# Binding the expert units' loads, and reads at the end, to the landing of earlier additions in a two-layer decoder kernel

## The chip, the core and the metric

The kernel runs on one core of a Trainium2 chip. A core has a matrix engine (TensorE, PE), a vector engine (VectorE, DVE), a scalar engine (ScalarE, ACT), GpSimd (POOL) and a sequencer for transfers (SyncE, SP). Each works through its own instructions in order, and they wait for each other and for transfers by semaphores. Transfers (DMAs) are issued by SP, ACT or POOL and are all carried out by the core's 16 DMA engines. The metric is the time of one execution on the device in microseconds; lower is better. The figure compared is the median of unprofiled runs.

## The reference, cut to what matters

The program is a decoder of two layers on 32 sequences of 100 tokens with 256 features (3,200 rows in all). Each layer has a self-attention, a cross-attention to a context and a mixture of experts. The change lies in the last of these stages, the mixture of experts of layer 1:

```
def _moe_forward(hidden_states, gate_weight, e_bias, w1, w2, w3, shared_gate, shared_up, shared_down):
    ...
    topk_idx, topk_w = _route(x, gate_weight, e_bias)          # 8 of 64 experts for each row
    ...
    xe = jnp.zeros((E, CAP, H), x.dtype).at[sorted_e, pos].set(tok_sorted, mode='drop')   # CAP = 256
    h = jax.nn.silu(jnp.einsum('ech,efh->ecf', xe, w1)) * jnp.einsum('ech,efh->ecf', xe, w3)
    ye = jnp.einsum('ecf,ehf->ech', h, w2)
    ...
    out = jax.ops.segment_sum(vals * flat_w[:, None], flat_t, num_segments=T)
    shared = jax.nn.silu(x @ shared_gate.T) * (x @ shared_up.T) @ shared_down.T
    return (out + shared).reshape(B, S, H)
```

An expert takes at most 256 rows; each of its outputs is weighted and added to the row that it came from. A shared part works on all rows. The kernel's output is the residual plus both.

## The kernel before, in words

**Units.** While layer 1's cross-attention ends, the routing puts each row into its place for each of its experts: POOL scatters rows, with their number and weights behind the 256 features (321 numbers, `XROW`), into `x1_d` in DRAM, 256 places to an expert (L1818). A list of the experts in use is computed (`listi`). Then `units` (L1992) works through 32 units in the order of that list: units 0 to 23 (`WHOLE`) are an expert's 256 places in two halves of 128, units 24 to 31 are the first half alone. What is left, if anything, is worked through by a second call behind a branch (L1921); it is not entered with this input.

**A unit's steps.** SP loads the expert's weights (`weights`, L1999 to L2003, 384 KB into a tile `we`, 12 of them) and its rows (`rows`, L2005 to L2016, 321 KB into a tile `xe`, 8 of them; half of that for a half unit). PE turns the rows (`expert_turn`, L2061), multiplies by the two first weights (`expert_hidden`), and two units later by the last one (`expert_add`); DVE writes the weighted result to a tile `ye` (L2109, 6 of them, each free again once its addition has landed), and POOL issues one indirect transfer for each half, which adds 128 rows of 256 numbers to a sum in DRAM (L2113). These are called additions here. There are 2 x 24 + 8 = 56.

**Two sums.** Additions go to two sums in DRAM in turn, even units to the first (`sum_d[0]`), odd ones to the second; the last three units, 29 to 31, all go to the second. An addition waits until those of the unit before on the same sum have landed, since two units may hold the same row (`self.depend(got, added.get(side, []), ...)`). The two halves of one unit don't wait for each other.

**The order of work.** The loop of `units` writes PE's order by hand: in step i it turns unit i, computes the hidden part of unit i-1, takes some steps of the shared part, and finishes unit i-2. SP's loads run ahead of it: weights 0 to 3, rows 0 to 4, weights 4 to 8 and rows 5 go first, and step i begins with rows i+6 and weights i+9. SP works in order; a load waits for a free tile, and for the eighth load before it, because eight semaphores go round. Rows also wait for `self.flag` (L1915), which says that the scatter has landed.

**The end.** x, the residual with the shared part, lies in SBUF as 25 tiles of 128 rows. When the units are done, each sum is read back in five chunks of five tiles (640 KB each, L1938), into `xnT` for the first sum and `wA` for the second, and DVE adds each chunk to x (L1941); after a chunk of the second sum ACT stores that part of x to the output (L1943). The chunks of the first sum wait for its last addition (unit 28), those of the second for `end`, a small POOL instruction (L2052) that waits for the last additions of both.

Of the kernel before, what the change touches and what calls it, by code (L numbers as in the profile page):

```python
# [13 lines left out]
ALU = mybir.AluOpType  # L14
# [6 lines left out]
NF = NT // P  # L21
# [100 lines left out]
class Kernel:  # L122
# [1764 lines left out]
    def l1_ffn(self):  # L1887
        nc, tc, a = self.nc, self.tc, self.a
        x = self.x
        with ExitStack() as st:  # L1890
            self.psum = st.enter_context(self.banks("l1f", s=3, t=3, m=2))
            pool = st.enter_context(tc.tile_pool(name="p1f", bufs=2))
            ep = st.enter_context(tc.tile_pool(name="e1f", bufs=2))

            self.wbs = self.wts.tile([P, 3584], F32, tag="wB", name="wB2")
            steps, route = self.shared, self.last_route
            with tc.manual_schedule(engines={mybir.EngineType.PE}):
                next(steps)
                next(steps)

                (used, _), = self.routes
                next(used)
                next(route)
                us = next(steps)
                next(used)
                next(route)
                us += next(steps)
                next(used)
                for _ in route:
                    pass  # L1910
                while us < FIRST1:
                    us += next(steps)

            flag = pool.tile([1, 1], F32, tag="flag", name="flag", bufs=2)
            self.flag = nc.gpsimd.memset(flag, 0.0)  # L1915
            self.depend(self.flag, self.sent1, "all rows are in their places")
            whole, first, second = (0, 1), (0,), (1,)
            units = [(u, whole) for u in range(WHOLE)] + [(u, first) for u in range(WHOLE, UNITS)]
            end, first = self.units(ep, units, steps)
            n = nc.values_load(self.listi[0:1, 2 * E1 : 2 * E1 + 1], min_val=0, max_val=E1)  # L1920
            with tc.If(n > 0):  # L1921
                units = [(u, second) for u in range(WHOLE, UNITS)] + [(u, whole) for u in range(UNITS, E1)]
                more, _ = self.units(ep, units)

                word = pool.tile([1, 1], F32, tag="word", name="word")
                branch = nc.sync.dma_start(word, self.sum_d[1][0:1, 0:1])
                self.depend(branch, [more.ins], "the units' sums")


            ends = [self.xnT.rearrange("p k n -> p (k n)"), self.wa1[:, : NF * D]]  # L1930
            ends = [t.rearrange("p (f d) -> p f d", f=NF) for t in ends]
            sums = [t.rearrange("(f p) d -> p f d", p=P) for t in self.sum_d]
            out = a["out"].rearrange("b t d -> (b t) d").rearrange("(f p) d -> p f d", p=P)

            for i, others in enumerate((first, [end.ins])):
                for f in range(0, NF, 5):
                    at = slice(f, f + 5)
                    got = nc.sync.dma_start(ends[i][:, at, :], sums[i][:, at, :])  # L1938
                    self.depend(got, others + [branch.ins], "the last sums")
                    tc.declare_no_dep(got.ins, group="behind", reason="SyncE has waited in the branch")  # L1940
                    nc.vector.tensor_tensor(x[:, at, :], x[:, at, :], ends[i][:, at, :], ALU.add)  # L1941
                    if i == 1:
                        nc.scalar.dma_start(out[:, at, :], x[:, at, :])  # L1943

    def shared1(self, first):

# [45 lines left out]
    def units(self, pool, units, beside=None):  # L1992

        nc, tc = self.nc, self.tc
        we, xes, xTs, hTs, added, tags = {}, {}, {}, {}, {}, {}
        self.after = None
        n_all = len(units)

        def weights(i):  # L1999
            we[i] = pool.tile([P, 768], F32, tag="we", name="we", bufs=12)  # L2000
            u = units[i][0]
            e = nc.sync.value_load(self.listi[0:1, E1 + u : E1 + u + 1], min_val=0, max_val=E1 - 1)
            nc.sync.dma_start(we[i], self.a["wexp"][bass.ds(e, 1)].rearrange("o p n -> p (o n)"))  # L2003

        def rows(i):  # L2005
            u, halves = units[i]
            t = xes[i] = pool.tile([P, 2, XROW], F32, tag="xe", name="xe", bufs=8)
            e = nc.sync.value_load(self.listi[0:1, u : u + 1], min_val=0, max_val=E1)
            if len(halves) == 2:
                at = self.x1_d.rearrange("(e s p) d -> e p s d", p=P, s=2)[bass.ds(e, 1)]  # L2010
                got = nc.sync.dma_start(t, at.rearrange("o p s d -> p (o s) d"))
            else:
                at = self.x1_d.rearrange("(e s p) d -> s e p d", p=P, s=2)[halves[0]][bass.ds(e, 1)]
                got = nc.sync.dma_start(t[:, 0, :], at.rearrange("o p d -> p (o d)"))
            if beside:
                self.depend(got, [self.flag.ins], "all rows are in their places")  # L2016

        with tc.manual_schedule(engines={mybir.EngineType.PE}):
            room = -3.0
            for i in range(4):  # L2020
                weights(i)
            for i in range(5):
                rows(i)
            for i in range(4, 9):
                weights(i)
            rows(5)
            for i in range(n_all + 2):
                if i + 6 < n_all:
                    rows(i + 6)
                if i + 9 < n_all:  # L2030
                    weights(i + 9)
                if i < n_all:
                    self.expert_turn(pool, i, len(units[i][1]), xes, xTs)
                if 0 <= i - 1 < n_all:
                    self.expert_hidden(pool, i - 1, len(units[i - 1][1]), we[i - 1], xTs, hTs)

                if beside and i < WHOLE:
                    room += 0.65
                    while room > 0:
                        took = next(beside, None)  # L2040
                        if took is None:
                            break
                        room -= took
                if 0 <= i - 2:
                    side = int(not beside or i % 2 == 1 or i - 2 >= n_all - 3)
                    self.expert_add(pool, i - 2, units[i - 2], we.pop(i - 2), tags, hTs, added, side, beside)
                if i < n_all:
                    tags[i] = self.expert_tags(pool, units[i], xes.pop(i))
            for _ in beside or ():
                pass  # L2050
        flag = pool.tile([1, 1], F32, tag="flag", name="flag_u", bufs=2)
        flag = nc.gpsimd.memset(flag, 0.0)  # L2052
        self.depend(flag, added.get(0, []) + added[1], "the units' sums")
        return flag, added.get(0)

    def expert_turn(self, pool, i, n, xes, xTs):
        nc = self.nc
# [181 lines left out]
```

## Time and profile before

| what | value |
|---|---|
| median of 3 unprofiled runs | 2843.68 us (2843.59 to 2845.27) |
| the profiled execution's own time | 2870.41 us |
| its span, first to last instruction | 2868.6 us |
| PE busy | 2756.2 us (96%) |
| DVE, ACT, POOL busy | 1773.2, 1391.4, 765.4 us |
| moved by the DMAs | 241.86 MB, 84 GB/s on average |
| `we` loads | 32, 384 KB each |
| `xe` loads | 24 of 321 KB, 8 of 160.5 KB |
| additions to the sums | 56, first POOL start 2717.35 us, last 2841.81 us |
| reads of the sums, stores of the output | 5 + 5 and 5, 640 KB each |

The profile is of one execution, with microseconds from the span's start. A line of a timeline gives start, duration, engine, source line, operation, tiles written and read, how often, and in brackets how long the engine sat idle before it and what ended that wait. SPq is the queue of SP's transfers; its durations are those of issuing, not of moving. In a table of stretches the columns are the stretch, its length, busy time (and instructions) of PE, of its weight loads, of DVE, ACT and POOL, then the granted clock of PE, the mean busy share of the DMA engines and GB/s. The chain that ended last is followed back from the last instruction to whatever released each step.

### The profile page before, as it was taken

The numbers are of one execution on the slowest core, as the hardware profiler recorded it, in microseconds if no ns is written. First come the engines' busy times: TensorE is split into PE (matmuls) and PEld (weight loads), VectorE is DVE, ScalarE is ACT, GpSimd is POOL, SyncE is SP. The second block draws the span as 40 slices with busy tenths as digits, with TensorE's granted clock in tenths as the row PEclk, the third lists the DMA queues.
The fourth block names the chain that finished last, engine by engine and source line by source line (L and its number), as shares of the span: only waits on it lengthen the run. The fifth ranks groups of instructions, "written<-read, shape, count | busy, mean of one in ns | idle before, by whom it ended". The sixth has DMA issues, their size and how long they took to land. (4 is left out here: it accounts for less than half of the span.)

```text
span 2868.6 us, 64252 instructions
## 1 busy us (share of the span) xinstructions
PE 2756.2 (96%) x24856; PEld 2133.5 (74%) x24856; DVE 1773.2 (62%) x5205; ACT 1391.4 (49%) x4210; POOL 765.4 (27%) x960
## 2 busy tenths in 40 slices
PE   8999999999999899999999999999999999999893
PEld 7888888777777656888886777777777777776582
DVE  7666766687888732222226877667676666776453
ACT  5554645677767511222223226556565556567120
POOL 3222212332222243222221230021211302223464
PEclk9999999999999899999999999999999999999997
DMA  7444333000000033665552210010000000000396
GB/s 249 131 134 162 133 141 120 22 16 16 16 16 16 10 124 125 199 210 207 197 201 87 79 42 9 7 50 21 18 15 9 15 9 14 10 11 6 96 269 161
DMA packets 133867, 241.86 MB, mean 84 GB/s; under 512 B 40714, under 2 KB 105925, under 8 KB 126768
## 3 DMA queue, kind: packets, MB, share of 16 engines
q1 hardware_dynamic: 103488, 143.53, 15.9%
q0 software_dynamic: 26784, 90.83, 9.8%
q8 instruction: 200, 3.28, 0.5%
q10 hardware_dynamic: 3280, 3.28, 0.3%
q14 instruction: 115, 0.94, 0.1%
HBM read 152.12 MB, written 111.18 MB: 92 GB/s over the span
## 5 line engine op out<-in xcount | busy, mean ns | idle before, releaser
L1818 POOL DMA_INDIRECT x_d<-xr,slot x200 | 194.9, 975 | 670.4 <-ACT eT L844 591.0
L178 PE MATMUL ps_t<-xnT,wA 128*128 128x200 f32 (+1 forms) x1608 | 321.9, 347 | 1.6 <-DMA wA<-in_wq 1.0
L178 PE MATMUL ps_t<-cT,q 128*128 128x361 f32 (+1 forms) x832 | 307.3, 472 | 0.0
L844 ACT COPY eT<-ps_t 124x384 f32<-124x384 f32 x400 | 191.2, 486 | 225.1 <-PE ps_t L843 219.6
L178 PEld LDWEIGHTS ps_t<-xnT,wA 128*128 128x128 f32 x1608 | 272.5, 191 | 30.1 <-issue 14.5
L834 ACT ACTIVATE wBx<-ps_t,m 128x361 f32<-128x361 f32 x400 | 227.4, 569 | 119.6 <-DVE m L831 109.2
L178 PE MATMUL ps_t<-xT,w 128*128 128x256 f32 (+1 forms) x1276 | 260.2, 363 | 0.7 <-ACT xT L172 0.7
L590 DVE TENSOR_REDUCE m<-ps_t 100x1 f32<-100x361 f32 x512 | 239.7, 524 | 19.3 <-PE ps_t L178 19.1
L178 PEld LDWEIGHTS ps_t<-xT,w 128*128 128x128 f32 x1276 | 223.6, 190 | 36.2 <-issue 9.3
L831 DVE TENSOR_REDUCE m<-ps_t 128x1 f32<-128x361 f32 x400 | 210.6, 527 | 60.3 <-PE ps_t L178 56.9
L843 PEld LDWEIGHTS ps_t<-ident,wBx 128*124 128x124 f32 x1200 | 150.2, 139 | 117.7 <-issue 70.7
L612 ACT ACTIVATE e<-ps_t 121x300 f32<-121x300 f32 x512 | 173.9, 426 | 123.1 <-PE ps_t L178 123.1
L384 ACT ACTIVATE e<-s,m 100x100 f32<-100x100 f32 x512 | 185.6, 364 | 66.2 <-DVE m L378 66.1
L843 PE MATMUL ps_t<-ident,wBx 128*124 128x128 f32 x1200 | 196.8, 275 | 3.6 <-DVE top L1758 2.3
L388 POOL TENSOR_TENSOR e<-e,rz 100x400 f32<-100x400 f32 x128 | 109.3, 855 | 323.7 <-PE ps_t L178 195.4
L178 PE MATMUL ps_t<-wA,cT 128*124 128x512 f32 x384 | 194.5, 594 | 0.0
L1465 DVE TENSOR_TENSOR h<-ps_t,g 128x256 f32<-128x256 f32 (+1 forms) x145 | 58.1, 402 | 188.6 <-ACT g L1464 178.8
L836 DVE TENSOR_SCALAR wBx<-wBx,sums 128x361 f32<-128x361 f32 x400 | 165.6, 414 | 9.4
L178 PEld LDWEIGHTS ps_t<-q,k 32*121 32x121 f32 x3072 | 129.0, 182 | 33.5 <-issue 7.1
L855 PEld LDWEIGHTS ps_t<-eT,v 124*64 124x64 f32 x3072 | 134.9, 137 | 15.2 <-issue 8.1
L1464 ACT ACTIVATE g<-ps_t 128x256 f32<-128x256 f32 (+1 forms) x145 | 52.8, 365 | 191.0 <-PE ps_t L178 165.9
L835 DVE RECIPROCAL sums<-sums 128x1 f32<-128x1 f32 x400 | 63.7, 159 | 126.0 <-ACT wBx L834 123.6
(335 smaller groups left out, 5500.9 us busy)
## 6 DMA issues: line engine op xcount, KB each, us to landing
x_d<-fill SPq DMA_DIRECT2D x16, 1284.0 KB
we<-in_wexp SPq DMA_DIRECT2D x32, 384.0 KB
cT<-in_ctxT SPq DMA_DIRECT2D x64, 186.0 KB
xe_d<-zero SPq DMA_DIRECT2D x8, 1028.0 KB
xe<-x_d SPq DMA_DIRECT2D x24, 321.0 KB
sum<-fill SPq DMA_DIRECT2D x10, 640.0 KB
yk<-y_d SPq DMA_DIRECT2D x25, 256.0 KB
xe<-xe_d SPq DMA_DIRECT2D x24, 257.0 KB
```

The lines of the kernel that those rows point to most:

```text
L178: self.nc.tensor.matmul(out, lhsT=l, rhs=r, start=(i == 0), stop=(i == n - 1))
L384: nc.scalar.activation(t[:, i, :], s[:, i, :], AF.Exp, bias=m[:, i : i + 1], accum_out=rz[:, i : i + 1])
L388: nc.gpsimd.tensor_tensor(t[:, h, :], t[:, h, :], self.last(rz[:, h], T), ALU.mult)
L590: got = nc.vector.tensor_reduce(m[:, j, o : o + 1], ps[r], AX.X, ALU.max, negate=True)
L612: nc.scalar.activation(t[:, r], ps[r].rearrange("p (c t) -> p c t", c=NKC), AF.Exp)
L831: self.after = nc.vector.tensor_reduce(m, ps, AX.X, ALU.max, negate=True)
L834: nc.scalar.activation(t, ps, AF.Exp, bias=m, accum_out=z)
L836: nc.vector.tensor_scalar(t, t, z, None, ALU.mult)
L843: nc.tensor.transpose(pt[:, c, :], es[n % 5][:, c * KC : (c + 1) * KC], self.ident)
L844: self.after = nc.scalar.copy(eT[:, :, o : o + P], pt)
L855: nc.tensor.matmul(pz[64 * j : 64 * j + 64, i, :], lhsT=v[:, c, h * 64 : (h + 1) * 64], rhs=eT[:, c, o : o + T], start=(c == 0), stop=(c = ...
L1818: got = nc.gpsimd.indirect_dma_start(out=self.x1_d[:, :], out_offset=bass.IndirectOffsetOnAxis(ap=slot[:, j, k : k + 1], axis=0), in_=xr[: ...
```

## The change

The loads move to the end of a step and run less far ahead: after unit i-2 is finished, step i issues rows i+5 and weights i+6 (before: rows i+6 and weights i+9, at the step's beginning). Weights 6 to 8 and rows 5, which were issued before the loop, are now issued in it. Rows i also wait for the landing of the additions of unit i-7, weights i for those of unit i-8, where there is such a unit. `units` returns the additions of every unit (`landed`) in place of those of the first sum's last unit.

At the end the ten reads come in another order: chunks 0, 1, 2 of the first sum, chunks 0, 1, 2 of the second, then chunk 3 of the first, 3 of the second, 4 of the first, 4 of the second. The first three wait for the landing of units 28, 29 and 30 respectively, all others for `end`. PE's, ACT's and POOL's instructions stay the same in number and order; DVE's and ACT's at the end follow the reads.

```
-            end, first = self.units(ep, units, steps)
+            end, landed = self.units(ep, units, steps)
+            open_at = [landed[len(units) - i] for i in (4, 3, 2)]
...
-            for i, others in enumerate((first, [end.ins])):
-                for f in range(0, NF, 5):
-                    at = slice(f, f + 5)
-                    got = nc.sync.dma_start(ends[i][:, at, :], sums[i][:, at, :])
-                    self.depend(got, others + [branch.ins], "the last sums")
-                    tc.declare_no_dep(got.ins, group="behind", reason="SyncE has waited in the branch")
-                    nc.vector.tensor_tensor(x[:, at, :], x[:, at, :], ends[i][:, at, :], ALU.add)
-                    if i == 1:
-                        nc.scalar.dma_start(out[:, at, :], x[:, at, :])
+            open_at += [[end.ins]] * 7
+            order = [(0, 0), (0, 1), (0, 2), (1, 0), (1, 1), (1, 2), (0, 3), (1, 3), (0, 4), (1, 4)]
+            for (i, f), others in zip(order, open_at):
+                at = slice(5 * f, 5 * f + 5)
+                got = nc.sync.dma_start(ends[i][:, at, :], sums[i][:, at, :])
+                self.depend(got, others + [branch.ins], "the last sums")
+                tc.declare_no_dep(got.ins, group="behind", reason="SyncE has waited in the branch")
+                nc.vector.tensor_tensor(x[:, at, :], x[:, at, :], ends[i][:, at, :], ALU.add)
+                if i == 1:
+                    nc.scalar.dma_start(out[:, at, :], x[:, at, :])
...
         def weights(i):
...
-            nc.sync.dma_start(we[i], self.a["wexp"][bass.ds(e, 1)].rearrange("o p n -> p (o n)"))
+            got = nc.sync.dma_start(we[i], self.a["wexp"][bass.ds(e, 1)].rearrange("o p n -> p (o n)"))
+            self.depend(got, landed.get(i - 8, []), "not in front of earlier units' sums")
...
         def rows(i):
...
             if beside:
                 self.depend(got, [self.flag.ins], "all rows are in their places")
+            self.depend(got, landed.get(i - 7, []), "not in front of earlier units' sums")
...
-            for i in range(4, 9):
+            for i in range(4, 6):
                 weights(i)
-            rows(5)
             for i in range(n_all + 2):
-                if i + 6 < n_all:
-                    rows(i + 6)
-                if i + 9 < n_all:
-                    weights(i + 9)
                 if i < n_all:
                     self.expert_turn(pool, i, len(units[i][1]), xes, xTs)
...
                     self.expert_add(pool, i - 2, units[i - 2], we.pop(i - 2), tags, hTs, added, side, beside)
+                    landed[i - 2] = added[side]
+                if i + 5 < n_all:
+                    rows(i + 5)
+                if i + 6 < n_all:
+                    weights(i + 6)
                 if i < n_all:
                     tags[i] = self.expert_tags(pool, units[i], xes.pop(i))
...
-        return flag, added.get(0)
+        return flag, landed
```

## The prediction

> **What bounds the kernel now.** I read the page first (TensorE, PE, is busy 96% of the span, so only a stage where PE waits can give time back), then the busy time by stretches for the last 150 us, then GpSimd's (POOL's) timeline there, the waits, SyncE's (SP's) own timeline, and the chain at the end. Stretches (PE, PEld, DVE, ACT, POOL busy, granted clock, DMA share, GB/s):
>
> ```profile
> 2721.00:2764.00 43.00, 42.71 (x209) 35.14 (x208) 25.19 (x73) 11.63 (x24) 27.88 (x18) 1.00 1.08 318
> 2764.00:2795.00 31.00, 31.00 (x162) 26.66 (x161) 19.32 (x57) 8.99 (x19) 22.59 (x15) 1.00 0.94 212
> 2795.00:2828.00 33.00, 22.39 (x123) 18.10 (x122) 13.39 (x49) 5.48 (x17) 27.05 (x18) 0.90 0.45 56
> 2828.00:2846.40 18.40, 2.37 (x11) 1.73 (x10) 7.76 (x9) 0.00 (x0) 6.36 (x5) 0.63 0.60 184
> 2846.40:2868.60 22.20, 0.00 (x0) 0.00 (x0) 8.60 (x6) 0.00 (x0) 0.00 (x0) 0.50 0.88 296
> ```
>
> PE works without a gap until 2795, then idles and its clock falls, while POOL is at its densest. The units end on POOL's additions. POOL's timeline:
>
> ```profile
> 2737.12 1.54 POOL L2113 DMA_INDIRECT sum<-ye,ids  x1 [2.25 <-DMA sum<-ye,ids]
> 2738.97 1.55 POOL L2113 DMA_INDIRECT sum<-ye,ids  x1 [0.30 <-DVE one L2090]
> 2755.85 1.54 POOL L2113 DMA_INDIRECT sum<-ye,ids  x1 [2.30 <-DMA sum<-ye,ids]
> ...
> 2812.70 1.55 POOL L2113 DMA_INDIRECT sum<-ye,ids  x1 [0.30 <-issue]
> ...
> 2834.73 1.54 POOL L2113 DMA_INDIRECT sum<-ye,ids  x1 [2.32 <-DVEq L1921]
> 2841.81 1.64 POOL L2113 DMA_INDIRECT sum<-ye,ids  x1 [5.53 <-DMA sum<-ye,ids]
> ```
>
> An addition takes POOL 1.55 + 0.30 = 1.85 us. Until 2790 every second unit waits longer: it waits for the landing of the addition before it on its sum (two sums, taken in turn). Afterwards POOL runs at 1.85. SP and the chain:
>
> ```profile
> 2720.88 0.38 SPq L2011 DMA_DIRECT2D xe<-x_d  x1
> 2768.13 0.38 SPq L2011 DMA_DIRECT2D xe<-x_d  x1
> 2787.16 8.24 SPq L2014 DMA_DIRECT2D xe<-x_d  x3
> 2833.24 5.02 SPq L1938 DMA_DIRECT2D xnT<-sum  x5
> 2846.35 4.00 SPq L1938 DMA_DIRECT2D wA<-sum  x5
> ```
> ```profile
> 2834.73 6.34 DMA sum<-ye,ids
> 2841.11 0.69 issue
> 2841.81 4.32 DMA sum<-ye,ids
> ...
> 2848.88 11.91 DMA wA<-sum
> 2860.88 1.49 DVE x_sb L1941
> ```
>
> The loads are all issued by 2795, far ahead of the additions, which end at 2845. Unit 30's addition then takes 6.34 us beside five reads of the first sum, and the last 22 us are transfers alone.
>
> **Landings.** The trace's DMA records give 144 packets to each addition on POOL's queue. From POOL's start to the last packet an addition took 6.0 to 6.8 us around 2730, 4.4 to 5.7 around 2780, 3.3 to 3.5 from 2797 on with no load in flight, 2.6 where few rows are valid (the half units). A weights packet takes 121 ns, a rows packet 56 ns; over 16 engines a unit's weights are 128 x 121 / 16 = 0.97 us, its rows 256 x 56 / 16 = 0.90. Over 42 additions (the fifth on) a straight line fits: latency = 3.41 + 0.89 x (engine time of load packets that start 1 to 5 us after POOL's start), to 0.45 us.
>
> **Part 1, the gates on rows and weights.** They bind. Rows 7 went out at 2720.88 and may now only follow unit 0's landing, 2725.94 in this trace; rows 23 went out at 2768.13 and must follow unit 16's, 2795.70. No instruction of PE, ACT or POOL changes; SP issues the same 64 loads, each now waiting for POOL's semaphores. Behind a waiting rows load on SP stands the next weights load, bound to the same landing, so nothing is held that was not held already.
>
> The pace of whole units follows from the chain on one sum: two units take 1.85 (first addition) + latency of the second + 1.4 (last packet to POOL's next start; 1.0 to 1.9 in the trace). With pace T a 4 us window holds 4/T units' loads: latency = 3.41 + 0.89 x 1.87 x 4/T. Both together give T = 4.14 us, latency 5.0. Before, units 2 to 16 took (2790.46 - 2727.76)/14 = 4.48 and units 16 to 24, with no loads about, 3.71, which is POOL's floor (2 x 1.85). The work of loading beside additions is not removed, it is spread; the gain is that the eight units at the floor no longer leave slack unused. At the start about two loads fewer are queued in front of unit 0, whose latency goes from 6.7 to about 5, so unit 2 starts near 2726.1. Unit 24 then starts at 2726.1 + 22 x 4.14 = 2817.2, before 2820.1: **-2.9 us**. Bounds: the floor of 3.71 from unit 5 (PE delivers it at 2738.3) gives 2808.8, -11.3; the early latency kept throughout (5.9) gives T = 4.58, 2826.9, +6.8. I take the fit's value, as it holds for both densities of loads.
>
> What it could cost on PE: a unit's turn needs its rows, issued about 1.0 us after the landing seven units back and landed some 4.5 us later; the result two units older follows 3.3 us after that turn. Result k is so ready at the earliest 16 us after the start of unit k-5, and is wanted 5 x 4.14 = 20.7 after it. 4 us of cover; a step of the shared part (3.4 us on PE) uses nearly all of it. I price it at 0; if the cover is gone, each shared step costs up to 3.4.
>
> Half units: in the trace, units 24 to 27 follow at 1.85 with latency 2.63 and 1.07 to the next start, exactly twice 1.85. Now loads of rows 27 to 31 (half size) and weights 28 to 31 fall here: 1.42 us of engine time per unit, latency +0.89 x 1.42 = +1.26 once on each sum, and some 0.5 more for unit 26: **+1.8 us** (0 to +4).
>
> A rule speaks against a gain here. The row: under loads an addition's first packet came 4.0 us after POOL's start, without them 2.1. The Trainium skill, "DMA: Bandwidth & Descriptors", section "Queues, rings and completion order", says that an engine alternates between its queues, finishing a packet of about 9 to 17 descriptors before it switches; so an addition waits for one such packet whether two loads are queued or five, and thinning the queue buys nothing while any load is in flight. By that the whole-unit term would be 0 in place of -2.9 and the total +4.8, an estimate from that page.
>
> **Part 2, the reads at the end.** Reads of chunks 0, 1, 2 of the first sum follow the landings of units 28, 29, 30; chunks 3 and 4 move behind the end. Beside unit 30's addition (before: first packet 4.13 us after POOL's start, when two chunks had gone by, last 5.71) there are still chunks 0 and 1; only the interleaving with chunk 2 goes, about 1.0. Unit 31's took 3.75 and has chunk 2 beside it: 0.2 less. **-1.2 us** (-3.0, both at 2.6 + 1.1, to +0.5). SP waits in order here, but behind these reads stand only those that wait for the end.
>
> After the end seven reads follow instead of five. The records show 343 packets a microsecond for reads from 2850 to 2856 and 377 for the stores until 2865, without a gap: 2 x 640 packets / 343 = 3.7 us more, and the last read, DVE's 1.49 and store stand further back, 0 to 0.9 more. **+4.2 us** (3.4 to 4.6). DVE's two moved additions (2 x 1.49) lie beside the transfers.
>
> **Sum**, on the profiled execution: -2.9 + 1.8 - 1.2 + 4.2 = +1.9, its span 2868.6 to 2870.5. That run took 2870.41, 1.8 around the span; the median of the unprofiled runs is 2843.68, 26.7 lower. I carry the difference over: **2845.6 us**. About 0.2% (5.7 us) is what a measurement of this kernel can tell from no change, so this is no change; its own range is 2840 to 2851.
>
> **Rivals.**
> (a) *The additions are freed*: POOL at its floor from unit 5. -11.3 + 0 - 1.2 + 4.2 = -8.3, **2835**. For: the latency falls to 3.4 as soon as loads end. Against: it needs second additions at 2 x 3.71 - 3.25 = 4.2 us, and none from unit 2 to 15 but one (3.66 at 2764.95, a first one) came under 4.3 with loads about. Chance 0.20.
> (b) *The loads collide with the very additions they wait for* (slower): a landing releases rows, weights and POOL's next unit on that sum at once, so both reach the DMA engines together, each time. Latency 5.9 as around 2740, T = 4.58, +9.7 against the forecast: **2855**. Each 0.1 us of latency costs 22 x 0.05 = 1.1 us, so it is slower than 0.2% from a latency of about 5.4. For: additions at 2766.80 and 2770.95, caught by three loads, took 5.4 and 5.7. Against: per unit the engines have 1.87 us of loads in over 4, so half of the additions should find them idle. Chance 0.25.
> (c) *The moved reads are hidden* under the stores: total -1.9, **2842**. Against it the gapless rates above. Chance 0.05. That the gates do nothing is excluded by the two issue times above.
>
> **How the numbers follow.** Forecast 0.50 (of it 0.37 within 0.2%, 0.10 slower, 0.03 faster), (a) 0.20 faster, (b) 0.25 slower, (c) 0.03 within and 0.02 faster. Together faster 0.25, same 0.40, slower 0.35. The range 2836 to 2856 takes in (a) nearly and (b) to its price, leaving 0.1 on each side.
>
> **What would show it.** Right: rows loads spaced about 4.1 us through to 2815; POOL waiting on DMA about as often at unit 22 as at unit 8; PE idle in small pieces from 2730 on; unit 24's addition at 2814 to 2820; seven reads and five stores in some 27 us after the last landing (23.0 before). Wrong: POOL at 1.85 steps under loads (a); latencies over 5.4 or PE waiting for xe (b); under 25 us after the last landing (c).

## The result, and the profile after

| what | before | after |
|---|---|---|
| median of 22 runs each | 2844.54 us | 2849.94 us |
| lowest and highest | 2841.70, 2850.53 | 2845.18, 2862.24 |
| ratio of after to before | | 1.0019, 95% interval 1.0011 to 1.0026 |
| profiled execution | 2870.41 us | 2851.53 us |

The change costs 5.4 us (3.1 to 7.4 by the interval): 0.19%, just inside the 0.2% that the prediction took for no change, though the 22 runs do tell it from nothing. The forecast was 2845.6, its range 2836 to 2856.

The two profiled executions can't be compared by their spans. The one before reaches the flag ahead of the units at 2705.18 us, the one after at 2679.34: 25.9 us apart ahead of anything that was changed. Runs of the kernel before on other chips show the same two levels (last section). So all that follows counts from POOL's start of unit 0's addition, and the sections between are:

| section | before | after | difference | predicted |
|---|---|---|---|---|
| unit 0 to unit 24 | 102.77 | 102.68 | -0.1 | -2.9 |
| unit 24 to unit 27 | 5.59 | 8.51 | +2.9 | +1.8 |
| unit 27 to the last landing | 19.84 | 19.44 | -0.4 | -1.2 |
| last landing to the end of the span | 22.99 | 27.70 | +4.7 | +4.2 |

POOL's starts and the span are read from timelines, landings from the DMA records (144 packets to an addition). The four differences add to +7.1 for two single executions; the medians say +5.4.

Busy time by stretches, after (columns as before: PE, its weight loads, DVE, ACT, POOL, granted clock, DMA share, GB/s):

```profile
2691.00:2735.00 44.00, 39.83 (x185) 32.88 (x184) 22.74 (x68) 10.85 (x22) 31.41 (x21) 0.92 0.91 217
2735.00:2766.00 31.00, 28.27 (x131) 22.64 (x130) 15.76 (x47) 7.42 (x16) 21.40 (x14) 0.96 0.92 210
2766.00:2799.00 33.00, 26.75 (x145) 22.54 (x143) 17.12 (x56) 7.58 (x20) 24.62 (x16) 0.89 0.86 201
2799.00:2822.10 23.10, 10.71 (x64) 8.88 (x64) 9.73 (x25) 1.85 (x6) 9.51 (x7) 0.83 0.43 117
2822.10:2849.80 27.70, 0.00 (x0) 0.00 (x0) 11.94 (x8) 0.00 (x0) 0.09 (x1) 0.50 0.84 285
```

The loads did what the change says: GB/s is even at 217, 210, 201 where it fell from 318 to 56 before. But PE, which was busy but for 0.3 us from 2721 to 2795 before, now idles in every stretch, and its granted clock is 0.92 and 0.96 in the first two, where it was 1.00 before. The last stretch is the end: transfers alone for 27.7 us.

What the engines waited for between unit 0 and the end of the units (engine, tile and line; total us, times, longest), first before, then after:

```profile
DVE ye L2109 <- DMA sum<-ye,ids: 17.4, 10, 3.2
POOL sum L2113 <- DMA sum<-ye,ids: 13.8, 7, 5.5
PE ps_t L2061 <- DMA xe<-x_d: 0.3, 1, 0.3
```
```profile
POOL sum L2117 <- DVE ye L2113: 21.1, 8, 12.0
PE ps_t L2065 <- DMA xe<-x_d: 13.9, 8, 4.8
POOL sum L2117 <- DMA sum<-ye,ids: 9.6, 4, 4.4
```

Before, DVE waited for a free `ye` tile: PE and DVE were so far ahead that they filled all six. That wait has gone (0.9 us is left), and in its place PE waits 13.9 us for rows. POOL waits less for landings and more for results: of its 21.1 us, 12.0 are the wait for unit 0, which is there before too. The results' lead over POOL (POOL's start less the end of DVE's write of that unit's `ye`) grew to 16 us by unit 24 before; after, it lies between 0 and 4 us at most units up to the 22nd. A result is called late here where POOL stood ready and started right behind the write of `ye`.

SP's, PE's and POOL's timelines, after, at the place where this lead runs out:

```profile
2716.68 0.60 SPq L2005 DMA_DIRECT2D we<-in_wexp  x1
2723.14 0.38 SPq L2014 DMA_DIRECT2D xe<-x_d  x1
```
```profile
2722.06 1.03 PE L178 MATMUL ps_m<-we,he 128*128 128x256 f32 x4
2727.26 1.08 PE L2065 MATMUL ps_t<-ident,xe 128*128 128x128 f32 x4 [4.17 <-DMA xe<-x_d]
```
```profile
2728.69 1.55 POOL L2117 DMA_INDIRECT sum<-ye,ids  x1 [0.30 <-issue]
2734.72 1.54 POOL L2117 DMA_INDIRECT sum<-ye,ids  x1 [4.48 <-DVE ye L2113]
...
2806.68 1.55 POOL L2117 DMA_INDIRECT sum<-ye,ids  x1 [0.30 <-issue]
2812.67 1.54 POOL L2117 DMA_INDIRECT sum<-ye,ids  x1 [4.44 <-DMA sum<-ye,ids]
2818.69 1.55 POOL L2117 DMA_INDIRECT sum<-ye,ids  x1 [4.48 <-DVE x_sb L1943]
```

Rows 12 went out at 2723.14, though unit 5, whose landing they are bound to, had landed at 2717.85. In SP's instructions, nine reads of list entries into registers (`value_load`, for this unit and for later ones) stand between weights 12 and rows 12: the scheduler, which orders SP, had put later units' reads in front of the load that waits. They fill the time from 2717.32 to 2722.80, 0.61 us for each. PE waits 4.17 us for these rows, the first turn after it takes 1.08 us where later ones take 0.44 in the chain, and unit 10's addition starts 4.18 us late. Rows 20 go out at 2757.81 in the same way, behind eight reads, though unit 13 had landed at 2753.42. The last three lines are the end: units 29, 30 and 31 follow each other at 6.0 us, where before it was 3.9 and 7.1.

The chain that ended last, after:

```profile
2723.14 3.98 DMA xe<-x_d
2727.26 1.08 PE ps_t L2065 x4
...
2757.81 4.40 DMA xe<-x_d
...
2806.68 5.26 DMA sum<-ye,ids
2811.95 4.53 DMA xnT<-sum
...
2829.51 14.16 DMA wA<-sum
```

It runs over PE and these two loads in the whole units, and at the end over unit 29's addition, a read of the first sum and the last reads of the second.

First theory (A): the parts add up. The end costs +4.7 less 0.4, the half units +2.9, and the whole units would have gained some 3 us had SP's register reads not made rows late. Rivals: the gates cost everything because the loads meet the additions they wait for (B); the gates gain and the end costs more (C); PE has too little cover whatever SP does (D); the additions' own latency sets the pace and PE's waits cost nothing (E).

### The profile page after: what moved, and what is told of

It is laid out like the page before. It is cut to its first block, busy times and chain, and to the rows that moved or that the text cites. A ratio compares the mean times of both kernels' runs of the same rounds, so it can differ in the third digit from the quotient of the medians.

```text
span 2849.8 us, 64259 instructions
## 1 busy us (share of the span) xinstructions
PE 2748.8 (96%) x24856; PEld 2129.8 (75%) x24856; DVE 1772.4 (62%) x5205; ACT 1392.4 (49%) x4210; POOL 765.2 (27%) x960
## 4 chain that ended last, share of the span: by engine, by line
PE 84%; DVE 8%; DMA 3%; ACT 2%; issue 2%; POOL 1%; SPq 0%; DVEq 0%; POOLq 0%; ACTq 0%
PE ps_t L178 59%; PE ps_t L855 5%; PE ps_t L843 5%; PE ps_t L1486 4%; PE ps_t L868 3%; DVE m L590 3%; PE ps_s L178 2%; PE ps_t L395 1%; PE ps_t L621 1%; PE ps_t L253 1%; PE ps_m L178 1%; DVE zd L636 1%; DMA sum<-ye,ids 1%; DMA wA<-sum 1%; DVE x_sb L1368 1%
```

## Experiments

Each run is compared with the kernel before on the same chip. e1 to e4 ran on one chip; e5 to e8, e9 and e10, and e11 and e12 ran on three others, where the kernel before takes 2870 to 2871 us, so ratios are compared, not times. A difference in us behind a ratio is worked out from the ratio, and can be up to 1.5 us away from the difference of the two medians. Profiles are of one execution each, and unit 24's start is counted from unit 0's.

**e1, the bound loads alone.** The end is that of before.

```
-            open_at = [landed[len(units) - i] for i in (4, 3, 2)]
+            first = landed[len(units) - 4]
...
-            for (i, f), others in zip(order, open_at):
+            for i, others in enumerate((first, [end.ins])):
+                for f in range(0, NF, 5):
```

> The bound loads of the change with the reads at the end as before. Theory A (the change adds up by its parts; in the two traces the units up to the 24th cost -0.1 us, the half units +2.9, the additions of units 30 and 31 -0.4, the transfers after them +4.7): about +2.9, that is some 2847.5 us beside 2844.5 before; 23 us from the last landing to the end of the span. Rival B (the gates themselves cost all of the +5.4, by loads that meet the additions they wait for, and the end costs nothing): +5 or more. Rival C (the gates gain what the prediction said, and the end costs more than 4.7): -1 to -3.

Measured: 2846.28 against 2846.38 us, ratio 1.0001 (0.9992 to 1.0011). The bound loads cost nothing and bring nothing, within 3 us. B falls with its 5 or more. The interval goes from -2.3 to +3.1 us, so these runs alone rule out neither A's +2.9 nor a small gain as in C; C falls by e2, where the end costs less than C's 7. Unit 24 starts at 100.85, units 24 to 27 take 8.69.

**e2, the end alone.** Loads as before, the ten reads in the order of after.

```
-            end, first = self.units(ep, units, steps)
+            end, landed = self.units(ep, units, steps)
+            open_at = [landed[len(units) - i] for i in (4, 3, 2)]
...
+            order = [(0, 0), (0, 1), (0, 2), (1, 0), (1, 1), (1, 2), (0, 3), (1, 3), (0, 4), (1, 4)]
```

> The loads as before, the order of the ten reads as after. Theory A: -0.4 and +4.7, so about +4 us, 2848.5; 27 to 28 us from the last landing to the end of the span. Rival B: within 1 us of before. Rival C: +7 or more.

Measured: 2849.28 against 2846.38, ratio 1.0011 (1.0002 to 1.0020), +3.1 us (0.6 to 5.7); from the last landing to the end 28.12 us, from unit 27 to the last landing 19.72 (19.84 before). The stretch behind the last landing, to be held against the last one of before in the prediction:

```profile
2819.40:2847.60 28.20, 0.00 (x0) 0.00 (x0) 11.94 (x8) 0.00 (x0) 0.09 (x1) 0.50 0.83 279
```

Of the two parts, only the end has a loss that can be told from nothing. e1 and e2 add to +3.4; the change has +5.4 with an interval that reaches down to 3.1, so some 2 us may belong to both together and stay unassigned.

**e3, SP in the order of the program.** The changed kernel, with each register read right in front of its own load.

```
-        with tc.manual_schedule(engines={mybir.EngineType.PE}):
+        with tc.manual_schedule(engines={mybir.EngineType.PE, mybir.EngineType.SP}):
```

> The changed kernel with SP's instructions in the units kept in the order of the program, so that each read of a list entry into a register stands right in front of its own transfer, and no group of them between two gated loads. Theory A with its cause for the missing 2.9 us (up to nine such reads at 0.65 us each hold back rows 11, 12 and 20 although the unit they wait for has landed, PE waits for them): PE's waits for xe fall from 13.9 us to under 7, unit 24 starts 2 to 4 us earlier counted from unit 0 (102.7 in the change), the time is 2 to 4 us below the change, 2846 to 2848. Rival D (PE's waits come from too few units of cover, whatever SP does in between): waits over 11 us, and the time within 1 us of the change.

Measured: 2855.41 against 2846.38, ratio 1.0034 (1.0022 to 1.0046): not faster than the change (1.0019) but by the medians slower, though the two intervals just overlap. The profiled run, 2848.90, was the quickest of its six, 6.5 us under their median. Its waits (columns as above):

```profile
POOL sum L2117 <- DMA sum<-ye,ids: 15.0, 8, 4.5
PE ps_t L2065 <- DMA xe<-x_d: 13.9, 11, 3.2
```

The groups of register reads have gone, and with them the longest wait (3.2 in place of 4.8), but PE waits for rows as long in all, now in eleven pieces. Results were late by 1.3 us between units 2 and 24 where they were by 5.8 in the change (sum of those starts of POOL that came right behind the write of `ye`). But POOL's waits for landings rose from 9.6 to 15.0. So what theory A took for the cause was cured and brought nothing. Rival D has its waits of over 11 us, but not its time, within 1 us of the change.

**e4, the gates one unit looser.**

```
-            self.depend(got, landed.get(i - 8, []), "not in front of earlier units' sums")
+            self.depend(got, landed.get(i - 9, []), "not in front of earlier units' sums")
...
-            self.depend(got, landed.get(i - 7, []), "not in front of earlier units' sums")
+            self.depend(got, landed.get(i - 8, []), "not in front of earlier units' sums")
```

> The changed kernel with each gate one unit looser (rows wait for the landing eight units back, weights nine), which gives PE one more unit, 4.2 us, of cover. SP's groups of register reads stay, at other places. Theory A and rival D both: PE's waits for xe fall under 5 us and unit 24 starts 2 to 4 us earlier than in the change. If instead the additions' own latency under loads sets the pace and PE's waits cost nothing (rival E): PE's waits fall and unit 24 starts where it did, 102 to 103.5 us after unit 0; time within 1 us of the change.

Measured: 2852.72 against 2846.38, ratio 1.0022 (1.0013 to 1.0031), like the change.

```profile
PE ps_t L2065 <- DMA xe<-x_d: 14.0, 10, 3.2
POOL sum L2117 <- DMA sum<-ye,ids: 13.7, 6, 4.4
```

PE still waits 14 us, so its waits did not fall as every theory had it; but no result was late any more (results lay 1.5 to 10.6 us ahead of POOL from unit 2 to 24), and unit 24 started at 103.34 all the same. That speaks against A and D, and it is what E says of the pace. A count over the runs so far: POOL's starts lay over its own step of 1.85, summed from unit 2 to 24, by 13.7 us before, 13.4 in e2, 13.7 in the change, 11.9 in e1, 12.3 in e3 and 14.2 in e4. The later kernels with two sums have 11.0 (e5), 12.5 (e6) and 16.4 (e8): 11.0 to 13.7 with loads as before, 11.9 to 16.4 with bound loads. Binding the loads did not lower it.

**e5, five reads early, bound.** Loads as before; chunks 2, 3 and 4 of the first sum are all bound to unit 30's landing, none is moved behind the end.

```
+            open_at = [landed[len(units) - i] for i in (4, 3, 2, 2, 2)]
+            open_at += [[end.ins]] * 5
+            order = [(i, f) for i in (0, 1) for f in range(5)]
```

> The loads as before; at the end all five chunks of the first sum are read ahead of the last landing, chunk 0 bound to unit 28's landing, chunk 1 to 29's, chunks 2, 3 and 4 to 30's; then the five of the second sum. Theory A (the two moved reads cost 4.7 us after the last landing, and their relief of the last additions is worth 0.4): 23 us from the last landing to the end of the span, some 1 to 2 us more for unit 31's addition, which now has three chunks beside it; in all 0 to +2 us against before, 2845 to 2848. Rival (it is the binding of chunks 0 to 2 that costs, not the two moved reads): +3 or more, as in the run with the end alone, with 23 us after the last landing and the loss ahead of it.

Measured: 2873.16 against 2871.25, ratio 1.0005 (0.9996 to 1.0014), +1.4 us (-1.1 to 4.0); 22.94 us after the last landing, 22.33 from unit 27 to it (19.84 before). The end is back at 23 as soon as the two reads are back in front of it. Ahead of it the binding takes 2.2 us from unit 30's addition (3.47 in place of 5.71) and gives 2.4 to unit 29's (5.20 in place of 2.83) and 2.7 to unit 31's (6.49 in place of 3.75).

**e6, all reads after the last landing.**

```
+            open_at = [[end.ins]] * 10
+            order = [(i, f) for f in range(5) for i in (0, 1)]
```

> The loads as before; all ten reads after the last landing, in turn from the first and the second sum. Prices what reads beside the last additions cost, and what a read after the end costs. Theory A: with no read beside them the additions of units 29 to 31 take 2.6 us and 1.1 to the next start, so from unit 27's start to the last landing 13.7 us or a little more (19.8 before); after it five more reads at 1.87 to 2.35 us, 32 to 35 us to the end of the span (23.0 before). In all +3 to +6, 2849 to 2852. Rival (the last additions are slow for another reason than the reads): 18 us or more to the last landing, in all +8 or more.

Measured: 2877.65 against 2871.25, ratio 1.0017 (1.0008 to 1.0026), +4.9 us. POOL at its end:

```profile
2834.88 1.55 POOL L2116 DMA_INDIRECT sum<-ye,ids  x1 [0.30 <-issue]
2839.89 1.54 POOL L2116 DMA_INDIRECT sum<-ye,ids  x1 [3.46 <-DVEq L1922]
2843.67 1.55 POOL L2116 DMA_INDIRECT sum<-ye,ids  x1 [2.24 <-DMA sum<-ye,ids]
```

Units 29, 30 and 31 follow each other at 5.0 and 3.8 us. With no read beside them, unit 27 to the last landing takes 16.29 (19.84 before), so five reads cost the last additions 3.5 us together, 0.7 each. The 13.7 that was expected was missed: with no read about, unit 29's addition still took 3.29 us in place of 2.6, and unit 30 started 1.7 us behind its landing in place of 1.1; why isn't known. Behind the end:

```profile
2846.10:2879.40 33.30, 0.00 (x0) 0.00 (x0) 14.93 (x10) 0.00 (x0) 0.09 (x1) 0.50 0.88 296
```

The five reads cost 33.26 - 22.99 = 10.3 there, 2.05 each. A read is three times cheaper beside the additions. (The two sections of this profile give +6.7, the runs +4.9 with an interval of 2.3 to 7.5.)

**e7, three sums.** Before, with whole units on three sums in turn; the third sum is read back and added ahead of the first.

```
-        self.sum_d = [dram.tile([NT, D], F32, tag=f"sum{i}", name=f"sum{i}") for i in range(2)]
+        self.sum_d = [dram.tile([NT, D], F32, tag=f"sum{i}", name=f"sum{i}") for i in range(3)]
...
+                    if beside and i - 2 < WHOLE:
+                        side = (i - 2) % 3
...
+            ends = [ends[0], ends[1], ends[1]]
...
-            for i, others in enumerate((first, [end.ins])):
+            for i, others in ((2, third), (0, first), (1, [end.ins])):
```

> Before, with a third sum: whole units go to three sums in turn, half units as before; the third sum is read and added ahead of the first. It tests what the pace of the whole units hangs on. Theory A (not on loads beside an addition but on the chain on one sum, latency and start; in all runs so far 11.9 to 14.2 us over POOL's own step of 1.85 between units 2 and 24, whatever the loads): those 13.7 us fall under 5, unit 24 starts at 90 to 96 us after unit 0 in place of 102.8; five more reads and 7.5 us of DVE's work, most of it beside the half units, give some of it back: -3 to -10 us, 2835 to 2842. Rival (PE would then be the bound, late results of 5 us or more): unit 24 after 98, time within 2 us of before or above.

Measured: 2862.22 against 2871.25, ratio 0.9966 (0.9952 to 0.9979), -9.8 us. POOL's timeline, one piece from the whole units and one from the end:

```profile
2741.87 1.55 POOL L2116 DMA_INDIRECT sum<-ye,ids  x1 [0.30 <-DVE he L2082]
2743.72 1.55 POOL L2116 DMA_INDIRECT sum<-ye,ids  x1 [0.30 <-issue]
2745.57 1.55 POOL L2116 DMA_INDIRECT sum<-ye,ids  x1 [0.30 <-DVE ye L2112]
...
2810.53 1.55 POOL L2116 DMA_INDIRECT sum<-ye,ids  x1 [0.38 <-DVE ye L2112]
2816.96 1.55 POOL L2116 DMA_INDIRECT sum<-ye,ids  x1 [4.88 <-DVE ye L2112]
```

POOL runs at its own step from unit 6 to 24; unit 24 starts at 90.74, and the 13.7 us over POOL's step have shrunk to 1.7. The additions themselves are slower here than in any kernel with two sums (5.28 us in the mean of units 2 to 23, against 4.68 before and 4.61 after), and up to unit 24 it doesn't matter. So with loads as before the pace of the whole units hung on the chain on one sum, and PE could follow at POOL's step. Some of the gain goes back: five more reads meet units 25 and 26 (7.2 us each), and unit 27 waits for 25.

**e8, the bound loads alone, SP in the order of the program** (e1 with the edit of e3).

> The bound loads alone (end as before) with SP in the order of the program. The run with SP in order and the change's end was 5 us above the change in its median, though its profiled run was its fastest and showed a shorter stage (156.7 us from the first addition against 158.3). If SP's order itself costs time: 2850 or more, 4 us over the bound loads alone (2846.3), and the profile shows where. If that difference was of those six runs: 2844 to 2848.

Measured: 2876.97 against 2871.25, ratio 1.0015 (1.0006 to 1.0024): +4.3 us, where e1 had 0.3. SP's order seems to cost time with the end of before too: the two intervals overlap a little (up to 1.0011 in e1, from 1.0006 here), but e3 against the change points the same way. Unit 24 starts at 105.43, with no late result among 2 to 24.

**e9, the third sum only up to unit 14**, so that its reads start earlier.

```
-                    if beside and i - 2 < WHOLE:
+                    if beside and i - 2 < 15:
```

> As the run with three sums, but the third sum takes units only up to the 14th, the units from 15 on go to two sums as before, whose additions are quick enough there (3.5 us without loads in flight). The third sum's five reads can so start some 25 us earlier, beside whole units with slack rather than beside units 25 and 26, whose additions took 7.2 us each in the run with three sums and held unit 27 back by 4.6. Theory A: units 24 to 27 take 5.6 us again (10.2 there), unit 24 starts at 90 to 94; -10 to -15 us against before (-9.0 there). Rival (the reads only meet other additions): unit 24 after 95, -5 to -9.

Measured: 2868.98 against 2870.35, ratio 0.9990 (0.9980 to 1.0000): most of the three sums' gain is gone. The reads went out 82.4 us after unit 0 (92.2 in e7), not 25 us earlier but 10, and met whole units 21 and 22 (up to 7.3 us); unit 24 starts at 96.65. The rival's mechanism and its mark (unit 24 after 95) hold, its price of -5 to -9 us hardly: -2.9 us was measured (-5.7 to 0.0). The profile has the rest behind unit 27, from where the last landing took 24.57 us (20.08 in e7).

**e10, three sums and the bound loads of the change.** e1 with the edits of e7.

> The three sums with the bound loads of the change (end as before plus the third sum's reads). It asks what the binding costs once the chain on one sum no longer covers it. Theory A (the binding takes PE's lead over POOL away: results lay 8 to 16 us ahead of their additions from unit 8 on before, 0 to 4 in the change, and only the chain on one sum hid that): results come late for 5 to 12 us between units 2 and 24, unit 24 starts at 95 to 101, time 4 to 10 us above the run with three sums and loads as before, about -5 to +1 us against before. Rival (the binding costs nothing but its half units): unit 24 at 90 to 93, 0 to 3 us above that run.

Measured: 2868.61 against 2870.35, ratio 0.9997 (0.9988 to 1.0006), against 0.9966 without the binding (and 0.9970 in e12): the binding as a whole costs 8 us here. The profiled run was the quickest of its eleven (2865.01), so it shows only part: unit 24 at 93.05, results late by 4.0 us (1.7 without binding), one of them here:

```profile
2764.58 1.55 POOL L2120 DMA_INDIRECT sum<-ye,ids  x1 [0.30 <-DVE he L2086]
2768.51 1.54 POOL L2120 DMA_INDIRECT sum<-ye,ids  x1 [2.37 <-DVE ye L2116]
```

PE waited 11.2 us for rows, and the results' lead is 3 us or less at every unit up to the 23rd. Unit 24 starts 2.3 us later than in e7, which is what the late results add, and lies below the 95 to 101 expected; the time lies inside what was expected. The rest of what the profile shows isn't PE's lead: the third sum's reads went out 101.65 us after unit 0 (92.23 in e7) and met units 28 and 29 (7.1 and 6.5 us) in place of 25 and 26, so that unit 27 came 3.1 us sooner after unit 24 and the last landing 3.7 later after unit 27. Where the other 4 us of the median go isn't seen in this profile.

**e11, three sums, the third's reads bound one by one** to the landings of units 23 to 27.

```
+                    late = landed[WHOLE - 1 + f // 5] if i == 2 else []
-                    self.depend(got, others + [branch.ins], "the last sums")
+                    self.depend(got, others + late + [branch.ins], "the last sums")
```

> The run with three sums, its five reads of the third sum bound one by one to the landings of units 23 to 27 in place of all to unit 23's. No read is moved behind the end. It asks whether binding a read to a landing helps where nothing else changes. Theory A (a read beside an addition costs the additions some 0.7 us wherever it stands, as between the runs with five, three and no reads beside the last ones): units 25 and 26 take 4 to 5 us in place of 7.2, the ones after them take more; unit 27's start to the last landing longer by what 24 to 27 gain; within 2 us of the run with three sums, -7 to -11 us against before. Rival (spreading the reads frees the additions): 3 us or more below it, -12 or better.

Measured: 2863.52 against 2870.65, ratio 0.9975 (0.9966 to 0.9984).

```profile
2811.57 1.55 POOL L2119 DMA_INDIRECT sum<-ye,ids  x1 [1.00 <-DVE ye L2115]
2814.64 1.55 POOL L2119 DMA_INDIRECT sum<-ye,ids  x1 [1.53 <-DVE ye L2115]
...
2826.34 1.55 POOL L2119 DMA_INDIRECT sum<-ye,ids  x1 [4.96 <-issue]
2834.22 2.53 POOL L2119 DMA_INDIRECT sum<-ye,ids  x1 [6.33 <-DVE x_sb L1944]
```

Unit 27 starts 2.25 us sooner after unit 24 than in e12 (7.48 against 9.73), and the last landing comes 2.29 later after it (22.94 against 20.65). In this pair of profiles, binding a read to a landing moves the collision and removes none.

**e12, three sums again**, beside e11.

> The run with three sums once more, since only five runs stand behind its -9.0 us, and beside the run above on one chip. If -9.0 holds: -6 to -12 us. If it was of those five runs: -5 or less.

Measured: 2862.73 against 2870.65, ratio 0.9970 (0.9958 to 0.9982), -8.6 us. It holds; by the ratios this version is quicker than the kernel before and, with that, than the change (1.0019).

## Why the prediction came close, and where it failed

The time lies in the range, but of the sum of +1.9 two terms failed, two held in size, and the one priced at nothing held for another reason than was given. The errors of the four sections all point the same way, so that +1.9 became +7.1 in the profiles and +5.4 in the medians. That the time stayed in the range is due to the range, which took in rivals on both sides: 2849.94 lies about halfway between the forecast and the 2855 of rival (b).

- **Whole units, -2.9: failed.** The step was the pace of 4.14 us, from a latency of 5.0 for every addition and 1.4 us from last packet to next start. The gain at the start came, and was larger than taken: unit 2 starts 7.5 us after unit 0 in four of the five kernels with two sums and bound loads, against 9.4 to 10.4 with loads as before, where 1.7 was taken. But the pace came out at 4.33 in the change, 4.24 to 4.45 in the four others with bound loads, and 4.12 to 4.22 in the four with loads as before, so the binding slowed it and the gain was used up. Both sizes in the chain were too small. Second halves whose successor on the same sum had to wait took 5.1 to 5.4 us in the five kernels with bound loads. From their landing to the next start it was 1.5 to 1.8 us in e3, e4 and e8, where hardly a result was late; the 1.9 of the change holds its two late results and is 1.35 without them.

  One reason for the slower additions may be how the loads lie. The step spread them evenly; in the traces the five kernels have 2.1 to 2.5 us of load packets beside these second halves and 1.4 to 1.7 beside the others, which took 3.8 to 4.2. (That is by the packets' recorded times. By the 121 and 56 ns that the prediction counted, the change has 1.71 and 1.34, and the prediction 1.81.) In units 2 to 13 of the kernel before the two groups have 2.7 and 2.5. This resembles rival (b)'s mechanism, a landing that releases the loads and the next addition on that sum together, at part of its price. It isn't shown: sorting the units by whether the next one waited picks the slow additions by itself, and no run moved the loads by half a period with all else equal.
- **PE's cover, priced at 0: the price held, the cover did not.** PE waited 13.9 us for rows, and 5.8 us of results came late. One reason was SP: "nothing is held that was not held already" missed the register reads that the scheduler put in front of waiting loads. But e3 and e4 took most of this lateness away and gained nothing: POOL's waits for landings rose from 9.6 to 15.0 and 13.7. Two limits lay at nearly the same length, so the price of 0 came out by luck; the lead of 16 us that PE had before was slack that the binding could use up. e10 shows that a price appears once the chain on one sum is gone: 2.3 us of late results, within the 8 us that the binding costs there in all.
- **Half units, +1.8: held in size.** +2.9 in the change, +1.3 to +3.2 in the four others with bound loads. Collisions explain it as foreseen: units 25 and 27 waited for the landings of 23 and 25.
- **Ahead of the end, -1.2: failed.** -0.4 in the change, -0.1 in e2. The step took chunk 2 from unit 30's addition and left unit 29's out; but chunk 0, bound to unit 28's landing, goes out 1.0 us behind unit 29's addition (2807.68 and 2806.68), which took 4.93 us in place of 2.83. e5 shows the same exchange, and e11 one like it. The additions of 29 to 31 stand in a chain on one sum, so each collision counts in full whichever of them meets it.
- **After the end, +4.2: right, somewhat small.** +4.7 in the change and +5.1 in e2. Rival (c), reads hidden under the stores, is out. (Its total of -1.9 takes off 3.8 us where the term is 4.2; nothing hangs on that.)
- **Rival (a), the additions freed:** out. The mean latency of units 2 to 23 was 4.61 after and 4.68 before: the same loads are spread, not removed. Three sums reach POOL's step in another way, with slower additions.

Of the prediction's own signs, the 27 us with seven reads behind the last landing came (27.70), and PE idling in pieces; but so did a sign of rival (b), PE waiting for `xe`. Unit 24, at 102.68 us after unit 0, came at the very end of what was given for it (97 to 103).

The rule weighed in the prediction, from the Trainium skill, "DMA: Bandwidth & Descriptors", section "Queues, rings and completion order", that an engine alternates between queues, from which thinning a queue was to buy nothing, gave 0 for the whole units and +4.8 in all; +5.4 was measured, so it came nearer than the fit. Its reason isn't borne out as simply: in each of the nine kernels with two sums, a straight line over 42 additions rises by 0.55 to 0.88 us for each us of load packets (by their recorded times) that start 1 to 5 us after POOL's, so more load beside an addition did go with a longer one.

The sum of the sections for the change, +7.1, is 1.7 above the difference of the medians, and e1's sections would give +2.8 where its runs give 0.3. Between the four profiles with loads as before, unit 24's start alone varies from 100.0 to 102.8. So a term under 2 us can't be settled from one execution each; the end's is settled by e2, e5 and e6 together.

## What to carry to other kernels

Before spreading transfers to spare an operation, ask whether that operation's latency or a chain of dependences sets the pace: here a third target for the additions brought 9 us although each addition became slower, while evening out the loads brought nothing. A transfer bound to a landing starts together with whatever else that landing releases; here the collisions changed their place, and the lead of the engines behind the bound loads was spent. At an end that consists of transfers, a read moved from beside a latency-bound chain to behind it costs its whole length (2.05 to 2.6 us here against 0.7).

## What the runs showed of the hardware that was not expected

- From chip to chip the kernel before differs by more than anything that was tried: medians of 2844.54 and 2846.38 us in the first two comparisons, 2870.35 to 2871.25 in the three that ran on other chips. The difference lies ahead of the units (the flag at 2678 to 2680 us against 2703 to 2709); the stage itself has nearly the same length. The profiled execution before, with its flag at 2705, fits the second kind, and so do the 26.7 us that the prediction carried over. Each chip was used on one occasion, so chip and occasion can't be told apart, and what differs isn't known.
- A read of a list entry into a register costs SP 0.61 us in the change, and reads for later loads can stand in front of a load that waits; behind nine of them one load went out 5.3 us after the landing that it was bound to, where the prediction reckoned with 1.0.
- With the register read behind the wait in place of ahead of it, a load follows the one in front 1.15 us later in place of 0.6, and by the medians that order cost 4 us (e8 against e1), with the first halves of additions at 4.89 us in place of 4.53. Why so small a shift should cost so much was not settled.
